# Layer 1 attention: the transposes of the last task's exponentials move ahead of this task's scores in each unit

## The chip, the cores and the metric

The kernel runs on one core of a Trainium2 chip. The metric is the device time of one execution in microseconds (us), measured outside the profiler; the profile is a separate execution of the same program.

## What is computed

A two-layer decoder over x of 64 sequences x 128 positions x 256 features. Layer 0 is a state-space block, a cross attention and a recurrent cell; layer 1 is a self attention, a second cross attention over `ctx_1024`, and a mixture of 8 experts with a shared expert. Only the self attention of layer 1 is touched:

```python
def _L1_attn_ref(x, w_q, w_k, w_v, w_o, g):      # x: the layer-normed input
    x_norm = _rms_norm(x, g)
    q = (x_norm @ w_q)...   # 16 heads of 16
    k = (x_norm @ w_k)...   # 4 key heads, each shared by 4 query heads
    v = (x_norm @ w_v)...
    qkt = einsum('brkqa,bkca->brkqc', q5 * rf, k * rf) / 16
    attn = softmax(qkt, axis=-1)
    s = einsum('brkqc,bkca->brkqa', attn, v)
    o = s @ w_o
    return s + o
```

## The kernel before

The 64 sequences are 16 groups of four. The program runs in four phases, each with its own on-chip buffers: the state-space block; cross attention and recurrence of layer 0; everything of layer 1 up to the routing (the phase of this change, called phase three here); the experts. All data are 32-bit floats.

In phase three, work is written as generators that yield. `run_units` (L62 on) keeps them in a heap ordered by (unit, priority, index). A generator that yields `(n, p)` is resumed n units later with priority p; within a unit the lower number goes first, and with equal numbers the older task. Inside `tc.manual_schedule` the order in which instructions are issued is the order in which each of the four compute engines executes them, so priorities are the instruction order of every engine. There is no other reordering.

One attention task is one sequence (b) and one half of its heads (c = 0 or 1): 8 heads, in two halves i of four heads. A new task begins every unit, so in every unit five tasks are at five different steps. What one unit U issues for attention, in the order before, by priority:

- 0: for a c = 1 task four units old, ScalarE copies `prs` out of PSUM (L324); for the task beginning now with c = 0, GpSimd builds the block-diagonal keys `kbd` (L349).
- 1: the task two units old. TensorE makes the scores `s0` and `s1` (L264), VectorE their row maxima `mx0` and `mx1` (L270), ScalarE the four exponentials of half 0 with their row sums (L282, here "e0").
- 2: for older c = 1 tasks VectorE adds the output to x (L335, odd units) or makes `oT` (L327, even units); then, for the task three units old, TensorE transposes the exponentials of the last unit, `pt0` and `pt1` (L294, 4 transposes each), ScalarE copies `pt0` to `eT0` (L296), VectorE copies `pt1` to `eT1` (L298), and in odd units VectorE takes the reciprocal of the row sums (L301) and ScalarE spreads it as `rd` (L303). This is the block that the change moves.
- 4: ScalarE's four exponentials of half 1 for the task two units old (L282, "e1").
- 5 and 6: the other work of the phase ("fill" below): the norms, projections and transposes of a group's inputs (`self_inputs`), the second cross attention and the routing (`cross_and_route`), and scatters of rows to DRAM (L958).
- 7: in even units TensorE's output projection `pr` (L331), which needs `oT`.
- 8: TensorE's attention-times-values `av` (L312), 16 small matmuls that need `eT0` and `eT1`; in odd units two transposes of `rd` behind it (L319).

The fill repeats every 8 units, one group. Units are named u0 to u7 below, by unit number modulo 8. The PSUM banks that matter, `s0`, `s1`, `pt0`, `pt1` and `av`, have one buffer each: the new `s1` must wait until the e1 of the task before has read it. The score matmuls of the two halves use 64 rows of the TensorE array each, rows 0 to 63 and 64 to 127.

`attention` is also used by the cross attention of layer 0 in phase two, with its own priorities for the fill.

Of the kernel before, what the change touches and what calls it, by code (L numbers as in the profile page):

```python
# [46 lines left out]
def last(ap, n):  # L47

    shape = list(ap.shape)
    return ap.unsqueeze(len(shape)).to_broadcast(shape + [n])  # L50
# [28 lines left out]
def tile_decoder(ctx: ExitStack, tc: tile.TileContext, a: dict, out: bass.AP):  # L79
# [13 lines left out]
    def load_rows(pool, name):  # L93

        return load(pool, name, a[name].rearrange("(c p) m -> p c m", p=P))
# [155 lines left out]
                start=(k == 0), stop=(k == 1),  # L251
            )

    def attention(g, b, c, work, ps, got, q, keys, values, wo):

        kb = keys()
        yield 2, 1
        ss = [ps.tile([P, 4, P], F32, tag=f"s{i}", name=f"s{i}") for i in range(2)]  # L260

        for i in range(2):
            rows = slice(i * 64, i * 64 + 64)
            nc.tensor.matmul(  # L264
                ss[i], lhsT=q()[rows], rhs=kb[rows, :, :], start=True, stop=True
            )

        mx = [work.tile([P, 4], F32, tag=f"mx{i}", name=f"mx{i}", bufs=2) for i in range(2)]
        for i in range(2):
            nc.vector.tensor_reduce(mx[i], ss[i], AX.X, ALU.min)  # L270
        e, eT = (
            [work.tile([P, 4, P], F32, tag=f"{n}{i}", name=f"{n}{i}", bufs=2) for i in range(2)]
            for n in ("e", "eT")
        )
        if c == 0:
            got["den"] = work.tile([P, 16], F32, tag="den", name="den", bufs=4)
        den = got["den"]

        def exponentials(i):
            for h in range(4):  # L280
                at = c * 8 + i * 4 + h
                nc.scalar.activation(  # L282
                    e[i][:, h, :], ss[i][:, h, :], AF.Exp, bias=mx[i][:, h:h + 1], scale=-1.0,
                    accum_out=den[:, at:at + 1],
                )

        exponentials(0)
        yield 0, 4
        exponentials(1)
        yield 1, 2  # L290
        for i in range(2):
            pt = ps.tile([P, 4, P], F32, tag=f"pt{i}", name=f"pt{i}")
            for h in range(4):
                nc.tensor.transpose(pt[:, h, :], e[i][:, h, :], ident)  # L294
            if i == 0:
                nc.scalar.copy(eT[i], pt)  # L296
            else:
                nc.vector.tensor_copy(eT[i], pt)  # L298
        if c == 1:

            nc.vector.reciprocal(den, den)  # L301
            rd = work.tile([P, 16, 16], F32, tag="rd", name="rd", bufs=2)
            nc.scalar.copy(rd, last(den, 16))  # L303
        yield 0, 8

        if c == 0:
            got["av"] = ps.tile([P, 4, P], F32, tag="av", name="av")
        av = got["av"]
        for odd in range(2):
            for j in range(4):  # L310
                h = 2 * j + odd
                nc.tensor.matmul(  # L312
                    av[j * 32:j * 32 + 32, c, :],
                    lhsT=values(h), rhs=eT[h // 4][:, h % 4, :], start=(odd == 0), stop=(odd == 1),
                )
        if c == 1:

            for k in range(2):
                nc.tensor.transpose(  # L319
                    av[:, 2 + k, :], rd[:, 8 * k:8 * k + 8, :].rearrange("p h e -> p (h e)"), ident  # L320
                )
            yield 1, 0
            prs = work.tile([P, 2, P], F32, tag="prs", name="prs", bufs=2)
            nc.scalar.copy(prs, av[:, 2:4, :])  # L324
            yield 0, 2
            oT = work.tile([P, 2, P], F32, tag="oT", name="oT", bufs=2)
            nc.vector.tensor_tensor(oT, av[:, 0:2, :], prs, ALU.mult)  # L327
            yield 0, 7
            pr = ps.tile([P, T], F32, tag="mm", name="pr")
            for k in range(2):  # L330
                nc.tensor.matmul(  # L331
                    pr[:, :D], lhsT=oT[:, k, :], rhs=wo[:, k, :], start=(k == 0), stop=(k == 1)
                )
            yield 1, 2
            nc.vector.tensor_tensor(X[g][:, b, :], pr[:, :D], X[g][:, b, :], ALU.add)  # L335

    def values_of(work, n, i):

        v = work.tile([P, n, 64], F32, tag=f"v{i}", name=f"v{i}")
        nc.gpsimd.memset(v[:, :, 16:48], 0.0)  # L340
        return v
# [5 lines left out]
    def block_diagonal(work, k, mask, bufs):  # L347
        kb = work.tile([P, 4, P], F32, tag="kbd", name="kbd", bufs=bufs)
        nc.gpsimd.tensor_tensor(out=kb, in0=mid(k, 4), in1=last(mask, P), op=ALU.mult)  # L349
        return kb  # L350
# [211 lines left out]
    with phase_pool("work1", "left") as work, phase_pool("ps1", space=PSUM) as psp:  # L562
        ps = PsumPool(psp, {"mm": 8})
        got = {}
# [13 lines left out]
    lwq, lwk, lwv, lwo = (load_rows(w3, n) for n in ("lwq", "lwk", "lwv", "lwo"))  # L578
# [82 lines left out]
    def cross_attention(g, b, c, work, ps, got):  # L661
        tb = slice(b * P, (b + 1) * P)
        v = got["v"][(g * G + b) % 3]
        yield from attention(
            g, b, c, work, ps, got, lambda: got[g, "qT"][c][:, tb],
            lambda: block_diagonal(work, got[g, "kT"][c][:, tb], turned, 3),
            lambda h: v[:, 4 * c + h // 2, h % 2 * 32:h % 2 * 32 + 32], xwo,
        )
# [60 lines left out]
    with phase_pool("work2", "left") as work, phase_pool("ps2", space=PSUM) as psp:  # L729
        ps = PsumPool(psp, {"mm": 3, "s0": 1, "s1": 1, "pt0": 1, "pt1": 1, "av": 1})  # L730
        got = {"c2": c2, "v": [values_of(work, 8, i) for i in range(3)]}
# [72 lines left out]
    def self_attention(g, b, c, work, ps, got):  # L804
        qT, kT, v = got[g]
        tb = slice(b * P, (b + 1) * P)

        def keys():
            if c == 0:
                got["k", b] = block_diagonal(work, kT[:, tb], head, 3)  # L810
            return got["k", b]

        yield from attention(
            g, b, c, work, ps, got, lambda: qT[:, c, tb], keys,
            lambda h: v[:, b * 2 + h % 4 // 2, h % 2 * 32:h % 2 * 32 + 32], lwo,
        )

    def wide_attention(g, work, ps):
# [207 lines left out]
    with phase_pool("work3", "left") as work, phase_pool("ps3", space=PSUM) as psp:  # L1026
        ps = PsumPool(psp, {"mm": 3, "s0": 1, "s1": 1, "pt0": 1, "pt1": 1, "av": 1})
# [31 lines left out]
        for k in range(2):  # L1059
# [5 lines left out]
        got = {"full": base, "v": [values_of(work, G * 2, i) for i in range(2)]}  # L1065
        tasks = [(8 * g, 5, self_inputs(g, work, ps, hc, got)) for g in range(NG)]
        tasks += [(8 * g + ATTEND + 11, 5, cross_and_route(g, work, ps, got)) for g in range(NG)]
        tasks += [
            (8 * g + ATTEND - 2 + 2 * b + c, 0, self_attention(g, b, c, work, ps, got))
            for g in range(NG) for b in range(G) for c in range(2)  # L1070
        ]
# [8 lines left out]
    with phase_pool("work4", "left") as work, phase_pool("ps4", space=PSUM) as psp:  # L1080
        ps = PsumPool(psp, {"mm": 5, "dn": 3})
# [323 lines left out]
```

## Time and profile before

| what | value |
|---|---|
| median of 3 executions | 3118.29 us (3117.29 to 3120.63) |
| the profiled execution, its own time | 3180.57 us |
| its span, first to last instruction | 3178.8 us |
| mean granted TensorE clock in it | 0.968 |
| TensorE busy, whole span | 94% |
| VectorE, ScalarE, GpSimd busy | 60%, 59%, 44% |
| first score matmul of phase three | at 1819.1 us |
| last exponentials of its attention | at 2644.2 us |

The profiled execution is 62 us longer than the median. In the profile each row names an engine (PE is TensorE, PEld its weight loads, DVE is VectorE, ACT is ScalarE, POOL is GpSimd), a source line, the tile written and the tiles read. A wait is written as the idle time of an engine and the instruction whose end released it. A matmul's record lasts until its result is out, which overlaps the next matmul, so distances between starts are used for TensorE and not the durations.

### The profile page before, as it was taken

The page shows a single profiled execution, that of the slowest core. Times are in us where ns is not written, and L with a number is a line of the kernel's source. Part 1 is how long each engine was busy: PE and PEld are TensorE (multiplying, and loading weights), DVE is VectorE, ACT ScalarE, POOL GpSimd, SP SyncE. Part 2 cuts the span into 40 slices and gives each one's busy share as a digit, 9 for nine tenths or more (in the row PEclk, how much of TensorE's full clock was granted, in tenths as well). Part 3 has the DMA queues.
Part 4 walks back from the last instruction along what each step waited for, and adds up shares of the span by engine and source line. Part 5 has one row for each costly group of instructions (what it writes and reads, how often), then busy time and mean ns, then how long its engine had stood idle before and what let it go on. Part 6 is the DMA issues. An engine that isn't in the chain of part 4 may idle for free.

```text
span 3178.8 us, 54631 instructions
## 1 busy us (share of the span) xinstructions
PE 2984.9 (94%) x19022; PEld 2042.6 (64%) x19022; DVE 1892.9 (60%) x4891; ACT 1861.4 (59%) x6757; POOL 1406.1 (44%) x1268
## 2 busy tenths in 40 slices
PE   7999999996999999999999699999999997899884
PEld 3666666653777777777777456666666665688542
DVE  5677777753555555555555367777777774433344
ACT  3655555543677667766776277777777773233100
POOL 2667766674434343334332222434342422333554
PEclk8999999998999999999999799999999998899897
DMA  9990000001111111111110100111111111677443
GB/s 309 343 343 32 1 1 1 1 15 52 35 29 33 39 36 29 33 39 36 31 32 21 43 14 28 59 43 61 41 61 41 54 41 50 227 226 222 125 157 120
DMA packets 192245, 246.60 MB, mean 78 GB/s; under 512 B 24672, under 2 KB 156256, under 8 KB 191968
## 3 DMA queue, kind: packets, MB, share of 16 engines
q1 hardware_dynamic: 174000, 196.92, 19.9%
q0 software_dynamic: 17968, 46.18, 4.7%
q8 instruction: 150, 2.46, 0.3%
q14 instruction: 127, 1.04, 0.1%
HBM read 113.65 MB, written 127.93 MB: 76 GB/s over the span
## 4 chain that ended last, share of the span: by engine, by line
PE 75%; ACT 9%; DVE 6%; POOL 4%; issue 3%; another core or an unknown queue 1%; DMA 1%; SPq 0%; DVEq 0%; ACTq 0%; POOLq 0%
PE proj L241 17%; PE s L264 8%; PE pt L294 6%; PE pu L695 5%; PE pu L691 5%; PE av L312 4%; PE pgu L1198 4%; ACT e L282 4%; PE seg L519 2%; PE po L546 2%; PE pr L331 2%; PE pv L249 2%; PE py L531 2%; PE pd L1207 2%; ACT xn L215 2%
## 5 line engine op out<-in xcount | busy, mean ns | idle before, releaser
L282 ACT ACTIVATE e<-s,mx 128x128 f32<-128x128 f32 x2048 | 738.4, 396 | 382.4 <-DVE mx L270 382.4
L270 DVE TENSOR_REDUCE mx<-s 128x4 f32<-128x512 f32 x512 | 331.4, 684 | 462.7 <-PE s L264 452.4
L282 ACT ACTIVATION_READ_ACCUMULATOR e<-s,mx 128x1 f32 x2048 | 479.5, 234 | 0.0
L189 POOL TENSOR_TENSOR ln_rstd<-ln_ve,neghalf 128x4 f32<-128x4 f32 x80 | 82.0, 1025 | 698.1 <-DVE ln_ve L205 558.2
L264 PE MATMUL s<-kbd,qT 64*128 64x512 f32 x1024 | 333.3, 649 | 18.5 <-POOL qT L631 8.6
L294 PEld LDWEIGHTS pt<-consts,e 128*128 128x128 f32 x2048 | 220.8, 141 | 194.5 <-issue 145.2
L241 PE MATMUL proj<-xnT,win 128*128 128x512 f32 x640 | 303.0, 610 | 0.0
L294 PE MATMUL pt<-consts,e 128*128 128x128 f32 x2048 | 281.5, 281 | 0.0
L423 DVE SCALAR_TENSOR_TENSOR acc<-proj,convw,acc 128x508 f32<-128x508 f32 (+2 forms) x288 | 211.6, 735 | 61.9 <-ACT acc L414 59.5
L691 PE MATMUL pu<-xnTb,fx 128*128 128x128 f32 x1536 | 235.6, 276 | 1.2 <-DVE xnTb L682 1.2
L695 PE MATMUL pu<-c,fu 128*128 128x128 f32 x1536 | 234.5, 275 | 1.8 <-DVE c L726 1.8
L691 PEld LDWEIGHTS pu<-xnTb,fx 128*128 128x128 f32 x1536 | 208.0, 192 | 31.3 <-issue 23.9
L349 POOL TENSOR_TENSOR kbd<-kT,consts 128x512 f32<-128x512 f32 x192 | 202.3, 1064 | 4.7 <-PE s L264 4.1
L695 PEld LDWEIGHTS pu<-c,fu 128*128 128x128 f32 x1536 | 202.4, 192 | 2.4 <-DVE c L726 2.4
L241 PEld LDWEIGHTS proj<-xnT,win 128*128 128x128 f32 x640 | 115.1, 193 | 112.9 <-issue 108.0
L312 PE MATMUL av<-eT,v 128*32 128x128 f32 x4096 | 165.8, 280 | 12.7 <-ACT eT L296 12.5
L298 DVE COPY eT<-pt 128x512 f32<-128x512 f32 x256 | 174.2, 680 | 4.8 <-PE pt L294 4.8
L630 POOL TENSOR_TENSOR other<-other,consts 128x512 f32<-128x512 f32 x64 | 81.4, 1271 | 198.6 <-DMA other<-raw 198.6
L1261 POOL DMA_INDIRECT ys<-ys,t_yrow x128 | 123.6, 966 | 90.8 <-DVE x L1271 40.9
L189 POOL TENSOR_TENSOR rn_rstd<-ln_ve,neghalf 128x1 f32<-128x1 f32 x64 | 37.2, 581 | 278.3 <-ACT prs L324 190.6
L526 POOL TENSOR_TENSOR m<-m,gm 128x1024 f32<-128x1024 f32 x64 | 151.0, 2360 | 15.8 <-ACT m L520 15.8
L312 PEld LDWEIGHTS av<-eT,v 128*32 128x32 f32 x4096 | 96.7, 109 | 95.4 <-issue 33.0
(280 smaller groups left out, 6531.4 us busy)
## 6 DMA issues: line engine op xcount, KB each, us to landing
xs<-zeros SPq DMA_DIRECT2D x64, 1024.0 KB
xs<-xs SPq DMA_DIRECT2D x71, 256.0 KB
ys<-y SPq DMA_DIRECT2D x71, 256.0 KB
ctxT<-in_ctxT_dram SPq DMA_DIRECT2D x32, 512.0 KB
other<-raw SPq DMA_DIRECT2D x256, 64.0 KB
x<-in_x_dram SPq DMA_DIRECT2D x16, 512.0 KB
xo<-xo SPq DMA_DIRECT2D x64, 128.0 KB
xo<-xo SPq DMA_DIRECT2D x16, 512.0 KB
```

The lines of the kernel that those rows point to most:

```text
L241: nc.tensor.matmul(o[:m, :], lhsT=w[:, k, m0:m0 + m], rhs=rhs[k], start=(k == 0), stop=(k == 1))
L264: nc.tensor.matmul(ss[i], lhsT=q()[rows], rhs=kb[rows, :, :], start=True, stop=True)
L270: nc.vector.tensor_reduce(mx[i], ss[i], AX.X, ALU.min)
L282: nc.scalar.activation(e[i][:, h, :], ss[i][:, h, :], AF.Exp, bias=mx[i][:, h:h + 1], scale=-1.0, accum_out=den[:, at:at + 1],)
L294: nc.tensor.transpose(pt[:, h, :], e[i][:, h, :], ident)
L298: nc.vector.tensor_copy(eT[i], pt)
L312: nc.tensor.matmul(av[j * 32:j * 32 + 32, c, :], lhsT=values(h), rhs=eT[h // 4][:, h % 4, :], start=(odd == 0), stop=(odd == 1),)
L349: nc.gpsimd.tensor_tensor(out=kb, in0=mid(k, 4), in1=last(mask, P), op=ALU.mult)
L423: nc.vector.scalar_tensor_tensor(acc[:, :, k:], pv[:, :, :P - k], convw[:, conv, 3 - k:4 - k], acc[:, :, k:], ALU.mult, ALU.add,)
L526: nc.gpsimd.tensor_tensor(out=m, in0=m, in1=mid(gm, 8), op=ALU.mult)
L691: nc.tensor.matmul(pu[:, i, :], lhsT=fx[:, k, m], rhs=xnT[:, k, :], start=(k == 0), stop=False)
L695: nc.tensor.matmul(pu[:, i, :], lhsT=fu[:, k, m], rhs=got["c2"][:, k, :], start=False, stop=(k == 1),)
```

## The change

`attention` gets an argument `turn`, the priority of the block with the transposes. Layer 0 keeps 2. Layer 1 passes 0.5, so in each unit of phase three the block of L294 to L303 is issued after priority 0 and ahead of the scores (1).

```diff
-    def attention(g, b, c, work, ps, got, q, keys, values, wo):
+    def attention(g, b, c, work, ps, got, q, keys, values, wo, turn=2):
...
         exponentials(0)
         yield 0, 4
         exponentials(1)
-        yield 1, 2
+        yield 1, turn
         for i in range(2):
             pt = ps.tile([P, 4, P], F32, tag=f"pt{i}", name=f"pt{i}")
...
         yield from attention(
             g, b, c, work, ps, got, lambda: qT[:, c, tb], keys,
-            lambda h: v[:, b * 2 + h % 4 // 2, h % 2 * 32:h % 2 * 32 + 32], lwo,
+            lambda h: v[:, b * 2 + h % 4 // 2, h % 2 * 32:h % 2 * 32 + 32], lwo, 0.5,
         )
```

The instructions and their number stay the same. By engine, the order at the head of a unit changes like this:

| engine | before | after |
|---|---|---|
| TensorE | s0 s1, pt0 pt1, fill, pr (even), av | pt0 pt1, s0 s1, fill, pr (even), av |
| VectorE | mx0 mx1, x add or oT, eT1, reciprocal (odd), fill | eT1, reciprocal (odd), mx0 mx1, x add or oT, fill |
| ScalarE | prs (even), e0, eT0, rd (odd), e1, fill | prs (even), eT0, rd (odd), e0, e1, fill |
| GpSimd | unchanged | unchanged |

No DMA is moved, and no queue of DMA issues.

## The prediction

> **What bounds the kernel now.** The page's first part says that TensorE is busy nearly throughout, so the question is what little idle time it has in phase three. The busy table by stretches narrows it: at a granted clock of 1.00, TensorE is busy 78.6 of 80 us, ScalarE only 60 to 64.
>
> ```profile
> PE 2984.9 (94%) x19022; PEld 2042.6 (64%) x19022; DVE 1892.9 (60%) x4891; ACT 1861.4 (59%) x6757; POOL 1406.1 (44%) x1268
> ```
> ```profile
> 2220.00:2300.00 80.00, 78.62 (x560) 50.24 (x560) 60.47 (x180) 60.36 (x260) 28.29 (x24) 1.00 0.14 46
> 2300.00:2380.00 80.00, 78.66 (x568) 51.36 (x567) 64.04 (x193) 64.29 (x270) 35.32 (x31) 1.00 0.17 57
> ```
>
> Busy hides stalls inside stretched records, so I then read the waits of the weight loads from 1900 to 2630 us (total, times, longest). `s` waits for the exponentials, which is the bank of s1; `av` waits for eT.
>
> ```profile
> PEld av L312 <- ACT eT L296: 19.9, 30, 1.0
> PEld s L264 <- ACT e L282: 16.0, 30, 0.5
> PEld av L312 <- ACT rd L303: 10.6, 14, 0.8
> ```
>
> The timeline shows how such a wait acts. First TensorE around u6 and u7 (start, length; I use distances between starts):
>
> ```profile
> 2335.93 0.44 PE L319 MATMUL av<-consts,rd 128*128 128x128 f32 x2
> 2336.30 1.13 PE L264 MATMUL s<-kbd,qT 64*128 64x512 f32 x4
> 2337.36 1.09 PE L294 MATMUL pt<-consts,e 128*128 128x128 f32 x8
> 2338.29 1.04 PE L227 MATMUL pt_ln<-consts,xn 128*128 128x128 f32 x8
> 2339.51 1.13 PE L331 MATMUL pr<-lwo,oT 128*128 128x256 f32 x4 [0.18 <-DVE oT L327]
> 2340.93 0.65 PE L312 MATMUL av<-eT,v 128*32 128x128 f32 x16 [0.29 <-ACT eT L296]
> 2341.50 1.96 PE L264 MATMUL s<-kbd,qT 64*128 64x512 f32 x4
> 2343.39 1.09 PE L294 MATMUL pt<-consts,e 128*128 128x128 f32 x8
> ```
> ```profile
> 2342.33 0.29 PEld L264 LDWEIGHTS s<-kbd,qT 64*128 64x128 f32 x2 [0.54 <-ACT e L282]
> ```
>
> In u6 both score halves take 1.06 together, because they run in different rows. In u7 s1 may not start until e1 of the last task is read; s0 runs alone, s1 runs alone behind it, and the pair takes 1.89. pt takes 0.93. From the end of e1's last read (2341.95 + 0.33 = 2342.28, ScalarE's timeline) to the fill at 2344.32 TensorE needs 2.04 us: 0.05 + s1 1.06 + pt 0.93. A period of 8 units is 52.8 us, and it has three stretched pairs: u3 (2315.89, 1.89), u4 (2322.34, 1.45), u7 (2341.50, 1.89). In u1 to u4 and from u5's e0 to u7, ScalarE runs without a gap and TensorE follows it; in between TensorE is the bound.
>
> **What the change does, part by part** (the profiled period from 2303.78 to 2356.59).
>
> 1. The scores no longer meet a bank in use: pt1 comes first and waits for e1, and once it has run both score banks are free, so the pair always takes 1.06. pt1 waits by head: the same kind of transpose, pt_ln, runs three of its four and waits only for the slice still missing:
>
> ```profile
> 2312.32 0.70 PE L227 MATMUL pt_ln<-consts,xn 128*128 128x128 f32 x3
> 2313.18 0.76 PE L227 MATMUL pt_ln<-consts,xn 128*128 128x128 f32 x5 [0.16 <-ACT xn L215]
> ```
>
> So behind e1 there is left: 0.05, one weight load 0.14 (mean of the L294 loads), one transpose 0.12 (0.93 / 8), a switch of 0.10 (point 5), the pair 1.06: 1.47 instead of 2.04, a gain of 0.57. If pt1 had to wait with all four heads, 0.35 of that is lost (0.22 left). It counts at u4 and u7: 2 x 0.57 = 1.14. At u3 I count nothing, because ScalarE goes on with `xnr` to 2318.4, which u3's transposes need anyway.
>
> 2. eT0 (0.47) and rd (0.31) leave the chain between e0 and e1. In u5 they move into idle time, and e0 pays for the later mx:
>
> ```profile
> 2331.70 0.37 ACT L282 ACTIVATE e<-s,mx 128x128 f32<-128x128 f32 x1 [2.59 <-DVE mx L270]
> 2333.09 0.60 ACT L296 COPY eT<-pt 128x512 f32<-128x512 f32 x1
> 2333.55 0.43 ACT L303 COPY rd<-den 128x256 f32<-128x256 f32 x1
> ```
>
> e0 begins 1.94 after the unit (2329.76); with pt ahead it is 1.94 + 0.93 + 0.10 = 2.97. 1.03 later less 0.78 gives e1 0.25 later. This goes through ScalarE's unbroken work in u6 to u7: loss 0.25. In u1, mx is held by VectorE's own fill (e0 at 2306.27): eT1 and the reciprocal, 0.76, now stand before it, and 0.78 leaves ScalarE: nothing. With that cover gone u1 would lose up to 0.76 more.
>
> 3. av no longer waits for eT0 or rd, which are 1 to 2 us earlier. Where it waited (u2, u6) the next unit's e1 wait follows, so nothing is counted; this stall becomes pt1's wait. Bounds: nothing, and 0.3 per period.
>
> 4. VectorE in even units: oT now follows eT1, mx0 and mx1, and `pr`, `av` and the next unit are queued behind oT on TensorE. From scores to the next scores: 1.16 (to mx0) + 1.20 (both mx) + 0.49 (oT to pr) + 0.95 + 0.58 + 0.93 + 0.10 = 5.41. In u6 the scores would start at 2336.75, so this path ends at 2342.16; that of e1 (2342.28 - 0.57 + 0.25, then 0.41 to the scores) at 2342.37. It is hidden by 0.2; without that cover it costs what it exceeds. GpSimd's keys come a unit or more early (2329.83 for 2341.50); it is 30 to 40% busy: nothing.
>
> 5. Order on TensorE itself. The Trainium skill, "TensorEngine Tiling (Array Packing)", Key Properties, speaks against the change: a change of the tiling mode drains the array. av is tiled by columns, the scores by rows, transposes by neither. In odd units the number of changes stays three; in even units av, s, pt, fill becomes av, pt, s, fill: four instead of three. The rows give a price: two transposes ahead of scores take 0.37 (2335.93 to 2336.30), where 8 of them ahead of full matmuls take 0.87 (u3), 0.22 for two: 0.15 for the change. pt behind scores takes 0.93 against 0.87: 0.06. I take 0.10. By the rule alone, all four even units would pay up to 0.15, 0.6 per period; by the rows only the TensorE-bound u0 pays beyond points 1 and 2: 0.10. pt straight ahead of scores appears nowhere in the trace; bounds 0 and 0.4 a unit.
>
> Sum per full period: 1.14 - 0.25 - 0.10 = 0.79 us. Full periods run from 1927.9 to 2560.9: twelve, 9.5 us. The period before them has two stretched pairs: 0.5.
>
> 6. The thin units 17 to 22, early in the phase, have almost no fill and are bound by the loop itself:
>
> ```profile
> 1853.35 1.96 PE L264 MATMUL s<-kbd,qT 64*128 64x512 f32 x4
> 1858.27 1.96 PE L264 MATMUL s<-kbd,qT 64*128 64x512 f32 x4
> 1862.98 1.74 PE L264 MATMUL s<-kbd,qT 64*128 64x512 f32 x4
> ```
>
> They take 4.7 to 4.9 now. After: odd 1.94 + 2.80 (8 exponentials) + 0.41 = 5.15, even 5.41, mean 5.28 against 4.81: 6 x 0.47 = 2.8 us lost. The last ten units, partly thin, have both effects; I count nothing.
>
> Total: 9.5 + 0.5 - 2.8 = 7.2 us against the profiled 3180.57. These stages ran at full clock, so I take the same 7.2 from the median: 3118.3 - 7.2 = 3111.
>
> **The rivals.** About 0.2% (6.2 us) is what a measurement of this kernel can tell from no change.
>
> A, the forecast: 3111, chance 0.5. Its own range: with 0.3 from point 3 and u3's pair counted in part (0.3), 1.4 per period, 14.5 in all: 3104. With u5's loss doubled, 0.54 per period: 3114.
>
> B, no change, 0.28: the stall is only renamed. pt1 waits with all four heads (gain 0.22 twice, less 0.35: 0.09 per period, 1.1) and the thin units take 2.8 back: 3120. For it: the exponentials still gate the same engine. Against: the two rows of pt_ln.
>
> C, slower, 0.22: the drain of transposes straight ahead of row-tiled scores. Place: L294 to L264, every unit. Price: 0.4 instead of 0.10, 0.3 more in the five TensorE-bound units (u4, u5, u7, u0, u1), 1.5 per period; 0.79 - 1.5 = -0.7, times 12 is -8.5, with the thin units (2.8 and 1.8 more for the drain) -13: 3131. It decides from 0.16 us above my 0.10 in each of the five; slower by over 0.2% from about 0.2 above. For it: the skill's rule, and that no row shows this pair. Against: 0.15 in the nearest row.
>
> That the change does nothing is excluded: it reorders three queues that run in order.
>
> **How the numbers follow.** A holds 0.48 faster and 0.02 same, B 0.23 same, 0.03 faster and 0.02 slower, C all slower: faster 0.51, same 0.25, slower 0.24. The range reaches from A's best, 3102 with the last units gaining, to 3127, which cuts C's far half.
>
> **What would show it.** Right: the pair takes 1.06 in every unit; PE's wait on e1 stands at pt with 1.5 from e1's end to the fill in u4 and u7; av's waits for eT and rd are gone; period 52.0; thin units near 5.3. Wrong: s starts over 1.1 after pt (C); pt1's four heads run together behind e1 (B); oT ends last in u6; u1's exponentials start late because eT1 stands ahead of mx.

## The result, and the profile after

The kernel after takes 3124.36 us (median of 20 executions, 3118.23 to 3129.35), the kernel before on the same chip 3119.59 (3117.29 to 3121.57): ratio 1.0016, interval 1.0009 to 1.0022. The forecast was 3111, so the sign is wrong; the time itself lies inside the stated range. The profiled execution of after took 3121.84, its span is 3120.1.

The page's first part and the busy table of the same two stretches as before (us, busy of TensorE, weight loads, VectorE, ScalarE, GpSimd, clock, DMA share, GB/s):

```profile
PE 2954.1 (95%) x19022; PEld 2025.4 (65%) x19022; DVE 1903.0 (61%) x4891; ACT 1872.9 (60%) x6757; POOL 1410.6 (45%) x1268
```
```profile
2220.00:2300.00 80.00, 77.83 (x564) 49.82 (x564) 63.35 (x182) 62.64 (x266) 28.70 (x24) 1.00 0.14 46
2300.00:2380.00 80.00, 77.70 (x569) 50.20 (x568) 65.16 (x193) 64.64 (x270) 35.50 (x31) 1.00 0.18 57
```

TensorE was busy 78.6 of 80 us here and is now busy 77.7 to 77.8, with some more matmuls in each stretch. It stalls less inside its records and more between them. The waits of its weight loads from 1900 to 2630 us say on what:

```profile
PEld pr L331 <- DVE oT L327: 15.3, 16, 2.5
...
PEld pt L294 <- ACT e L282: 8.1, 40, 0.2
...
PEld proj L241 <- DVE x L335: 5.4, 13, 0.7
```

The scores' wait for e1 (16.0 us in 30 waits before) is not in the list any more; the transposes' wait for e1 that takes its place is never longer than 0.2. The lines of av's waits for eT0 (19.9 us) are gone and those for rd (10.6) are down to one of 0.3. Idle time of the weight loader alone does not show that TensorE stood still, but here its matmuls agree: `av` now starts 1.06 after `pr`, where it was 1.42. Two waits for VectorE have grown: new is, in each u3, that of a projection for the x add of L335, and that of `pr` for oT was in the list of before with

```profile
PEld pr L331 <- DVE oT L327: 6.3, 14, 0.9
```

TensorE around u6 and u7, as shown of before:

```profile
2337.08 1.13 PE L264 MATMUL s<-kbd,qT 64*128 64x512 f32 x4
2338.14 1.09 PE L227 MATMUL pt_ln<-consts,xn 128*128 128x128 f32 x8
2339.91 1.13 PE L331 MATMUL pr<-lwo,oT 128*128 128x256 f32 x4 [0.68 <-DVE oT L327]
2340.97 0.65 PE L312 MATMUL av<-eT,v 128*32 128x128 f32 x16
2341.55 1.09 PE L294 MATMUL pt<-consts,e 128*128 128x128 f32 x8
2342.57 1.13 PE L264 MATMUL s<-kbd,qT 64*128 64x512 f32 x4
2343.63 1.12 PE L241 MATMUL proj<-xnT,lwq 128*128 128x512 f32 x2
```

The score pair of u7 takes 1.06 (2342.57 to 2343.63) instead of 1.89. The last read of e1 ends at 2341.86 + 0.33 = 2342.19 (ScalarE's timeline), so from there to the fill it is 1.44 us: 1.47 was predicted, 2.04 it was. A period of eight units takes 52.51 us instead of 52.81. That is a gain of 0.30 where 0.79 was predicted, 3.0 us over the thirteen periods from unit 25 to unit 129 (681.99 to 679.01, units counted from the start of the phase); the ends of the phase lose more than that.

### The profile page after: what moved, and what is told of

It reads as the page before. It is cut to its first block, busy times and chain, and to the rows that moved or that the text cites. A ratio compares the mean times of both kernels' runs of the same rounds, so it can differ in the third digit from the quotient of the medians.

```text
span 3120.1 us, 54702 instructions
## 1 busy us (share of the span) xinstructions
PE 2954.1 (95%) x19022; PEld 2025.4 (65%) x19022; DVE 1903.0 (61%) x4891; ACT 1872.9 (60%) x6757; POOL 1410.6 (45%) x1268
## 3 DMA queue, kind: packets, MB, share of 16 engines
q14 instruction: 127, 1.03, 0.1%
## 4 chain that ended last, share of the span: by engine, by line
PE 82%; DVE 6%; POOL 4%; ACT 4%; issue 3%; DMA 1%; SPq 1%; POOLq 0%; ACTq 0%; DVEq 0%
PE proj L241 17%; PE s L264 9%; PE pt L294 8%; PE pu L695 6%; PE pu L691 6%; PE av L312 4%; PE pgu L1198 4%; PE pr L331 4%; PE pv L249 4%; PE seg L519 2%; PE po L546 2%; PE py L531 2%; PE pd L1207 2%; PE pxo L249 2%; DVE mx L270 2%
## 5 line engine op out<-in xcount | busy, mean ns | idle before, releaser
L282 ACT ACTIVATE e<-s,mx 128x128 f32<-128x128 f32 x2048 | 730.3, 394 | 288.9 <-DVE mx L270 285.4
L264 PE MATMUL s<-kbd,qT 64*128 64x512 f32 x1024 | 297.4, 651 | 15.8 <-POOL qT L631 8.6
L294 PEld LDWEIGHTS pt<-consts,e 128*128 128x128 f32 x2048 | 224.8, 141 | 122.2 <-issue 101.3
L294 PE MATMUL pt<-consts,e 128*128 128x128 f32 x2048 | 285.7, 280 | 2.9 <-ACT e L282 2.3
L296 ACT COPY eT<-pt 128x512 f32<-128x512 f32 x256 | 159.3, 622 | 50.9 <-PE pt L294 50.0
L704 ACT ACTIVATE th<-pu,fb 128x128 f32<-128x128 f32 x384 | 115.4, 379 | 65.8 <-PE pu L695 65.8
```

The lines of the kernel that those rows point to most:

```text
L264: nc.tensor.matmul(ss[i], lhsT=q()[rows], rhs=kb[rows, :, :], start=True, stop=True)
L282: nc.scalar.activation(e[i][:, h, :], ss[i][:, h, :], AF.Exp, bias=mx[i][:, h:h + 1], scale=-1.0, accum_out=den[:, at:at + 1],)
```

## The experiments

Chips differ: the kernel before was measured again beside each batch of runs, and took 3120 us in three of the batches (the result above; runs 1 to 4; runs 13 to 16) and 3172 to 3178 in the other three (runs 5 to 8; 9 to 12; 17 and 18). They are called the 3120 chips and the 3175 chips below. Times are compared as ratios to the kernel before on the same chip, and traces by distances inside phase three. The runs are numbered in the order of their texts here. Two theories stood at the start: the thin units and the last units lose more than the full periods gain (so the old order there brings the gain out), or TensorE pays more for the order itself (so the loss is in the full periods too). A third one came out of run 5.

**The control, and the thin units apart.** First a second profile of the kernel before, then the old order in the first units, then the new order there alone:

```diff
-  ... lwo, 0.5,
+  ... lwo, 2 if g == 0 or (g == 1 and b == 0) else 0.5,     # run 2
+  ... lwo, 0.5 if g == 0 or (g == 1 and b == 0) else 2,     # run 3
```

> The kernel before again, unchanged, for a second profile, because its first profile carries long waits on an unknown queue near the end of phase three (7.1 us) and in the last phase. Theory clock (TensorE loses its full clock in the thin units 17 to 22 of the changed kernel and not before the change): no stretch at half clock between the first scores of phase three plus 25 us and the last scores. Theory switches (only the order on TensorE costs): the same trace. Both: a period of 52.8 us, first scores to unit 25 about 66.7 us.

> The block keeps priority 2 in the thin units (blocks in units 14 to 23) and has 0.5 from unit 24 on. Theory clock: the thin units' loss, larger in unprofiled runs than in the profile, is gone, the full periods' gain of 0.3 each stays: 3116 us, with a scatter as small as that of before (4 us). Theory switches (the loss lies in the full periods of the unprofiled runs, the thin units cost only the 0.8 us of their loop): 3123 to 3124, scatter as after.

> The mirror of it: priority 0.5 in the thin units alone, 2 from unit 24 on. Theory clock: 3125 to 3128 with the wide scatter of after (some 10 us), a stretch at half clock among units 17 to 22 of the profile. Theory switches: 3120 to 3121, scatter of before.

The control, a single execution on a 3120 chip, took 3121.17. Run 2: 3119.46, ratio 0.9996 (0.9989 to 1.0002), period 52.51. Run 3: 3122.78, ratio 1.0007 (0.9999 to 1.0015), period 52.85. From the scores of unit 13, with which the phase's attention begins, to those of unit 25 the control takes 65.65, run 3 67.34: the new order costs this stretch 1.7 us. The thin units are 5.10 long in odd and 5.49 in even units (before: 4.92 and 4.71). The 1.7 leans on the control: the clock is at half when the phase starts, and in unit 14 the control takes 7.06, but the profile of before and seven more of the old order take 8.01 or 8.02, with a mean clock of 0.50 in it instead of 0.58. Against those the loss would be 0.6. The profile of after takes 70.86 over the same stretch. 1.02 of that is only that its scores stand 1.02 later in their unit; 2.3 is one unit, unit 20, of 7.82 us instead of 5.49, and the busy table (columns as above) shows why, for after and for run 3:

```profile
1857.00:1865.00 8.00, 6.27 (x31) 3.13 (x32) 2.79 (x8) 3.95 (x20) 4.13 (x5) 0.57 0.00 0
```
```profile
1857.00:1865.00 8.00, 5.92 (x57) 3.10 (x53) 5.02 (x13) 5.14 (x25) 5.29 (x4) 1.00 0.00 0
```

The granted clock fell to half for 6.8 us, and 31 instead of 57 matmuls were run. This is not peculiar to one execution: the profiles of runs 9, 10 and 13, which have the same order in these units and were taken on chips of both kinds, show the same unit at 7.83 and the same 6.8 us at half clock. In each of the four it comes 30.7 us after the clock had come back to full at the start of the phase. In run 3, with the same order up to unit 23, the clock came back after 13.7 us at half and not after 10.2, and did not fall again. What makes it fall is not shown. The last units are the other half of what the ends cost: from unit 129 to unit 140 the control takes 64.82, run 2 and after 66.72: 1.9 us.

**Odd units only; full periods only.**

```diff
+  ... lwo, 0.5 if c == 1 else 2,                            # run 4
+  ... lwo, 0.5 if (1, 1) <= (g, b) and g < NG - 1 else 2,   # run 5
```

> The block has 0.5 only for tasks with c = 1, so only in odd units; even units keep scores first and so have three changes of tiling on TensorE as before. Theory switches: units u0 and u4 are back at 6.97 and 7.03 plus at most 0.05, the odd ones keep 0.05 more, the stretched pair of u7 is gone and that of u4 stays; period 52.5 to 52.7, thin units shorter than in after; 3117 to 3120. Rival oT path (the even units are held by oT and not by the order): u2 and u6 fall from 5.5 to 5.2 or less between scores and TensorE waits for e1 instead.

> Priority 0.5 only in the full periods (blocks from unit 24 to unit 133), 2 in the thin units at both ends. Theory ends (the full periods gain 0.3 each and the thin units at both ends give it back, at the start partly by a half clock): period 52.5, first scores to last exponentials 3 us shorter than before, 3116 to 3118. Theory full periods (unprofiled runs lose inside the full periods): not faster than before, 3120 to 3124.

Run 4: 3119.88, ratio 0.9999 (0.9990 to 1.0007), with executions from 3112 to 3126; its profile has a period of 52.30: odd units alone gain 0.51 a period, more than all units together, and the time does not show it. Run 5: ratio 1.0017 (1.0009 to 1.0026), where the thin units keep the old order and nothing should lose. Its period is 53.12 instead of 52.51, and all of the difference is in u3, which takes 7.18 instead of 6.57. So the same code has two lengths of u3. That was not in any of my theories; it is clearest in a second profile of the kernel after itself (below, run 9).

**u3, u4 and u7 apart.**

```diff
+  ... lwo, 0.5 if c == 1 and b in (0, 2) and 0 < g < NG - 1 else 2,                      # run 6
+  ... lwo, 0.5 if (b, c) in ((0, 1), (2, 1), (3, 0)) and 0 < g < NG - 1 else 2,          # run 7
```

> Priority 0.5 only in u3 and u7 of the full groups, where the score pair was stretched to 1.89 us; all other units keep the order of before. Theory switches (each extra change of tiling on TensorE costs 0.1 to 0.2 us in a unit where TensorE is the bound, and moving the block pays only where e1 is waited for): u1 and u5 are back at 6.54 as seen from fill to fill, period 51.8 to 51.9, 12 us faster than before, 3108 to 3110. Rival oT path (the gain comes from the block being early everywhere, because eT and av are early): period no shorter than with all odd units, 52.2, 3113 or more.

> As the one before, and u4 too, whose pair took 1.45 us. Theory switches: 0.39 of stretch against 0.2 of an extra change: period 51.6 to 51.8, 3106 to 3109. If u4 is not held by e1 any more once u3 has moved: 0.2 longer per period than without u4.

Ratios 0.9992 (0.9981 to 1.0003) and 0.9994 (0.9983 to 1.0005), periods 52.78 and 52.87, where 51.6 to 51.9 was expected. In run 6, from fill to fill, the steps of u6 and u7 together gain 0.54, those of u2 and u3 together lose 0.51: u7 gains and u3 loses as much. But this loss is the second length of u3 again. In the second and third full period, where VectorE's copy in u3 is on time, u2 and u3 take what they take in before (12.29 and 12.27 in the third); from the fourth on the copy is 0.9 late and they take 12.77 to 12.95 for 12.26 to 12.42. So by these two periods u3's block, moved together with u7's alone, costs nothing by itself.

**Dummy transposes against the half clock** (run 8). After, with ten transposes of the identity behind the scores of the first and last units, whose results nothing reads.

```diff
+        if warm:
+            pw = ps.tile([P, 4, P], F32, tag="mm", name="pwarm")
+            for j in range(warm):
+                nc.tensor.transpose(pw[:, j % 4, :], ident, ident)
```

> The changed kernel with ten extra transposes of the identity behind the scores in the thin units (tasks of group 0 from its third sequence, the first sequence of group 1, and group 15); their result is read by nobody. Theory clock: no stretch at half clock between units 17 and 23 nor among the last attention units, 2 to 3 us faster than the changed kernel without them (3121 to 3122), scatter halved. Theory loop only (the thin units lose by their chain and not by the clock): 3124 to 3125 with the scatter of after.

Ratio 1.0032 (1.0023 to 1.0042). The half clock did not appear in the thin units: from unit 13 to unit 25 it is 69.47 us in this profile, 70.83 in that of after on another of the 3175 chips (run 9). The kernel after was not measured on this chip, so what the dummies are worth in the time stays open.

**Who holds VectorE's copy in u3.** After again (run 9), and (runs 10 to 12) the scatters of a group's last three sequences one unit later, in the new order, in the old order and in that of run 6:

```diff
-                yield 1, 6
+                yield (2 if b == 0 else 1), 6
```

> The changed kernel again, beside the next three. Theory port (in u3 the copy eT1 on VectorE, now at the head of the unit, races with the second scatter of the unit before on GpSimd; where the scatter starts first, eT1 waits about 1 us until it ends): the period is either 52.5 us (eT1 of u3 starts at once) or 53.1 us (it starts 0.9 to 1.0 us late), and the time is 4 or 10 us above before accordingly. Theory clock and switches alone: always 52.5.

> The changed kernel with the second to fourth pair of row scatters of a group issued one unit later, so that no scatter stands at the head of u3 on GpSimd. Theory port: eT1 of u3 starts at once and the period is 52.5 or less on any chip; against the changed kernel without the shift 0 us where that already had 52.5, 7 us less where it had 53.1 (twelve periods of 0.6). Theory without port: no difference to the changed kernel.

> The control: the order of before with the same shift of the scatters. Theory port: eT1 of u3 does not wait in before (it comes behind both mx), so the shift gives nothing: within 2 us of before, period 52.8. If the shift is worth something by itself: faster than before by more than 3 us.

> Priority 0.5 only in u3 and u7 of the full groups, with the shift of the scatters. Theory switches and port: period 51.9 to 52.2, no loss in the thin units, 7 to 11 us faster than before. If the gain of u3 and u7 needs the other units too: period 52.5 or more, 3 us at most.

Ratios: after 1.0029 (1.0015 to 1.0044), shifted after 1.0078 (1.0061 to 1.0096), shifted before 1.0059 (1.0045 to 1.0073), shifted run 6 1.0049 (1.0036 to 1.0062). On this chip after lost more than in the result above, and its period was 53.06. Compare one u3 in the two profiles of the same kernel, VectorE first, of the profile that goes with the result:

```profile
2369.32 0.69 DVE L298 COPY eT<-pt 128x512 f32<-128x512 f32 x1 [0.80 <-PE pt L294]
...
2370.37 1.29 DVE L270 TENSOR_REDUCE mx<-s 128x4 f32<-128x512 f32 x2 [0.20 <-PE s L264]
2371.58 0.41 DVE L335 TENSOR_TENSOR x<-pr,x 128x256 f32<-128x256 f32 x1
```

and of the second profile, whose scores of this unit start at 2374.35 (those above at 2369.21):

```profile
2375.38 0.69 DVE L298 COPY eT<-pt 128x512 f32<-128x512 f32 x1 [1.71 <-PE pt L294]
...
2376.14 1.22 DVE L270 TENSOR_REDUCE mx<-s 128x4 f32<-128x512 f32 x2
2377.28 0.41 DVE L335 TENSOR_TENSOR x<-pr,x 128x256 f32<-128x256 f32 x1
```

The copy eT1 starts 0.11 after the scores in the first and 1.03 after them in the second, and maxima, x add and projection come late with it. "PE pt" is named as the releaser, but the transposes were as early as in the first. GpSimd in the two profiles:

```profile
2369.35 0.96 POOL L958 DMA_INDIRECT xs<-xnr,r_rows  x1 [0.30 <-issue]
```
```profile
2374.49 0.96 POOL L958 DMA_INDIRECT xs<-xnr,r_rows  x1 [0.30 <-issue]
```

Both scatters start 0.14 after the scores. In the first profile the copy was 0.03 us ahead and ran beside the scatter; in the second it starts when the scatter is over (2374.49 + 0.96 = 2375.45, within 0.07). It looks like a race for the first start, but the other periods speak against that. In the first profile again, another u3, where the scatter is 0.11 ahead of the copy:

```profile
2054.27 0.69 DVE L298 COPY eT<-pt 128x512 f32<-128x512 f32 x1 [0.94 <-PE pt L294]
```
```profile
2054.16 0.96 POOL L958 DMA_INDIRECT xs<-xnr,r_rows  x1 [0.30 <-issue]
```

Both run at their usual length. In the first full period with scatters of the second profile, the scatter starts 0.21 after the scores, 0.10 after the moment at which the copy starts elsewhere, and the copy is held all the same, to 1.05. What does divide the profiles is the chip: in those of after and run 2, on 3120 chips, the copy is on time in all eleven u3 with a scatter beside them; in those of runs 5, 8 and 9, on 3175 chips, it is late in all eleven. What differs between these chips is not shown. The weight load of the projection in the second profile waits 0.92 us for the x add, 0.35 in the first:

```profile
2377.74 0.30 PEld L241 LDWEIGHTS proj<-xnT,ym 128*128 128x128 f32 x2 [0.92 <-DVE x L335]
```

The Trainium skill, "SBUF — State Buffer", section "SBUF: two separate sides", has a rule that comes to mind: VectorE and GpSimd share a pair of ports by an exclusive lock, and whichever starts first keeps it for its whole instruction. The page names the VectorE instructions that take it: those in a mode that uses two ports, or with two inputs in SBUF against a GpSimd instruction that reads SBUF. The copy has one input, in PSUM, so by the page alone it is not expected to be held; and the order of starting does not decide here. So what holds it is not shown to be this lock.

The shift did take the scatter out of u3: shifted after has u3 at 6.56 again, on the same chip where unshifted after has 7.12. This pair of runs shows that the scatter holds the copy. But it pushed GpSimd's unbroken chain further into u5 and u6, with an instruction of VectorE on the other side of it (VectorE, then GpSimd, shifted after):

```profile
2402.27 3.90 DVE L212 SCALAR_TENSOR_TENSOR ln_off<-ln_mv,ln_inv 128x4 f32<-128x4 f32 x1
```
```profile
2403.78 2.36 POOL L766 TENSOR_TENSOR xo<-xo,hc 128x1024 f32<-128x1024 f32 x1
```

The tiny L212, 0.16 us in most units of the trace of after, lasts 3.90 and ends with GpSimd's addition (2406.17 and 2406.14); it has two inputs in SBUF and the addition reads SBUF, which is a pair that the page's rule names. If it is that lock, GpSimd kept it over three instructions in a row, since the record of L212 begins inside a scatter (2401.80 to 2402.77). eT1 and oT of u6 come 1.7 us later for it, and u6 takes 7.60 instead of 5.49; the old order with the shift has the same (6.94 instead of 5.20). So the shift moved one collision and made a larger one, in every order, and the times of these runs do not tell what u3 is worth.

**Without scatters, u7 alone, and all but u3.** All on one 3120 chip. Runs 13 and 14 leave the scatters out, in the new and the old order, so that no routed row is written and the experts see none.

```diff
-                nc.gpsimd.indirect_dma_start(out=XV..., in_=xn[:, b, :], in_offset=None)   # runs 13, 14
+  ... lwo, 0.5 if c == 1 and b == 0 and 0 < g < NG - 1 else 2,                            # run 15
+  ... lwo, 2 if (b, c) == (2, 1) else 0.5,                                                # run 16
```

> The kernel after with the row scatters of the routing (L958) left out: the routed rows are not written, so the experts compute on rows without tokens. Race theory (eT1 at the head of u3 waits for a scatter that GpSimd started just before): without scatters eT1 in u3 starts 0.04 us after pt1 in every period, u3 takes 6.57 us, a period 52.5, and the ratio to the same kernel in the old order (the run without scatters of the kernel before) is 0.999 to 1.001. Order theory (the loss comes from the order of TensorE and the thin units alone): period 53.1 as in the last profiles of the kernel after, ratio to the old order without scatters 1.003.

> The control: the kernel before with the same scatters left out (the routed rows are not written). Both theories: period 52.8, as with them, since in the old order no copy waits for a scatter; GpSimd's time falls by 128 instructions of about 1 us, and the time falls by at most a few us at the end of the phase.

> Only the block of u7 (c = 1, b = 0) of the full periods goes ahead of the scores. Race theory: u7 is free of scatters and has the larger part of the gain; the pair of u7 goes from 1.9 to 1.06, the period from 52.8 to 52.3 (0.53 from fill to fill), twelve or thirteen times: -6 us, ratio 0.998. Rival (a stall removed in u7 is only moved to the next u1 or u3): period 52.7 to 52.8, ratio 0.9995 to 1.0005.

> The kernel after with the block of u3 alone (b = 2, c = 1) back in its old place. Race theory: no copy stands ahead in the unit that has the scatter in front, so the period is 52.4 to 52.7 in every profile instead of 53.1 where the race is lost, and the time is about 6 us under that of the kernel after on a chip where it loses, ratio 1.000 to 1.001. Order theory: u3 was one of the units that gained, so the period is 53.1 or more and the ratio 1.003 or more.

| run | median us | ratio to before (interval) | period |
|---|---|---|---|
| 13, after without scatters | 3123.00 | 1.0009 (1.0001 to 1.0018) | 52.50 |
| 14, before without scatters | 3122.88 | 1.0010 (1.0003 to 1.0017) | 52.71 |
| 15, u7 alone | 3113.22 | 0.9981 (0.9972 to 0.9989) | 52.25 |
| 16, all but u3 | 3115.49 | 0.9982 (0.9976 to 0.9989) | 52.05 |

Without scatters eT1 starts 0.04 us after its transposes in every u3, u3 takes 6.56, and the two orders differ by 0.1 us, each to about 0.08%. For the scatter this is no further evidence, since in the profiles of the moved u3 on 3120 chips (after, run 2) u3 takes 6.56 with scatters too. That the old order did not get faster without the scatters, but 0.1% slower, was not expected and stays unexplained.

Run 16 is the one that surprised: its period is 0.46 shorter than that of after *with no collision in either trace*. So moving u3's block cost time from the start, and the scatter only adds to it. TensorE's weight loads in u3, of after:

```profile
2370.27 0.31 PEld L227 LDWEIGHTS pt_ln<-consts,xnr 128*128 128x128 f32 x3 [0.76 <-ACT xnr L215]
2370.80 0.14 PEld L227 LDWEIGHTS pt_ln<-consts,xnr 128*128 128x128 f32 x1 [0.22 <-ACT xnr L215]
2371.28 0.42 PEld L227 LDWEIGHTS pt_ln<-consts,xnr 128*128 128x128 f32 x4 [0.34 <-ACT xnT L229]
2372.05 0.30 PEld L241 LDWEIGHTS proj<-xnT,ym 128*128 128x128 f32 x2 [0.35 <-DVE x L335]
```

and of run 16:

```profile
2365.51 0.90 PEld L227 LDWEIGHTS pt_ln<-consts,xnr 128*128 128x128 f32 x8
2366.38 0.30 PEld L241 LDWEIGHTS proj<-xnT,ym 128*128 128x128 f32 x2
```

In the old order the transposes `pt` stand between the scores and this fill, just while ScalarE makes `xnr` and VectorE the maxima and the x add; when the fill comes, everything is ready and nothing waits. In the new order `pt` is done ahead, and the fill, straight behind the scores, waits twice for ScalarE (0.22 and 0.34) and then for the x add. (The 0.76 of the first line is no wait of TensorE's: the loader is idle that long while a pair of scores runs, in u3 of before too.) From the first of these transposes to the projection it is 1.77 us in after and 0.87 in run 16. The x add ends 1.16 + 1.21 + 0.41 = 2.78 us after the scores (to the maxima, the two maxima, the add), and the projection starts at 2.84. VectorE's copy is not in the way there: in the lines of u3 above it is over at 2370.01, and the maxima wait for the scores until 2370.37. From the end of e1 of u2 (where `xnr` begins) to the projection it is 3.45 in after and 3.12 in run 16 and before.

**TensorE's transposes alone, and the version the findings point to.** Run 17 moves only the transposes and leaves eT0, eT1, the reciprocal and rd in their old places; run 18 moves all but u3, in the full periods.

```diff
+        pt = [ps.tile([P, 4, P], F32, tag=f"pt{i}", name=f"pt{i}") for i in range(2)]     # run 17
+        for i in range(2):
+            for h in range(4):
+                nc.tensor.transpose(pt[i][:, h, :], e[i][:, h, :], ident)
+        if turn < 1:
+            yield 0, 2
+        nc.scalar.copy(eT[0], pt[0])
+        nc.vector.tensor_copy(eT[1], pt[1])
...
+  ... lwo, 0.5 if 0 < g < NG - 1 else 2,                                                  # run 17
+  ... lwo, 0.5 if 0 < g < NG - 1 and (b, c) != (2, 1) else 2,                             # run 18
```

> In the full periods only, TensorE's transposes alone go ahead of the scores; the copies eT0 and eT1, the reciprocal and rd stay where they were, behind the maxima and e0. VectorE theory (the gain of the score pairs is given back where eT1 and the reciprocal stand ahead of work that TensorE waits for: the x add in u3, oT in u2 and u6, and a scatter that blocks eT1): u3 starts its projection without a wait for the x add, no copy meets a scatter, u6 is under 5.4 us, and the period is 52.2 or less. Rival (what costs is that TensorE's scores come 1 us later, so that maxima and exponentials come later, whatever VectorE does): eT0 and rd now stand between e0 and e1 again, 0.78 us more in odd units, and the period is 52.8 or more.

> Every block of the full periods but that of u3 goes ahead of the scores; the first and last group and u3 keep the old order. By the trace of the kernel with only u3 put back the period is 52.05, so over twelve periods 0.75 x 12 = 9 us less than before, less some 0.5 us at the ends: ratio 0.9970 to 0.9976. Rival (what the thin units lost was in part lost by the full units around them): ratio 0.998, as with u7 alone.

Run 17: ratio 1.0061 (1.0047 to 1.0075), period 54.24. The theory that VectorE's copy ahead of the maxima is what costs foresaw 52.2 or less and fell; its rival, 52.8 or more, held. With no copy ahead the projection of u3 waits for the x add all the same. This u3 is not a clean case, since on this 3175 chip the maxima behind a scatter are late too, 1.61 after the scores (at 2379.73) instead of 1.16:

```profile
2381.34 1.29 DVE L270 TENSOR_REDUCE mx<-s 128x4 f32<-128x512 f32 x2 [2.34 <-PE pt_ln L227]
```

Most of the loss is elsewhere. With the copies behind, oT and eT0 are later still (TensorE in u6 of run 17, scores at 2346.31):

```profile
2349.48 1.13 PE L331 MATMUL pr<-lwo,oT 128*128 128x256 f32 x4 [1.01 <-DVE oT L327]
2350.90 0.65 PE L312 MATMUL av<-eT,v 128*32 128x128 f32 x16 [0.29 <-ACT eT L297]
```

`pr` starts 3.17 after the scores instead of 2.83, av another 1.42 later instead of 1.06, and u6 takes 6.25. So the copies early are a help that the new order needs. That what costs in it is the shorter stretch of work between the scores and whatever waits for their maxima rests on the lines of u3 above; no run adds other work there to test it.

Run 18: 3163.16 against 3171.93, ratio 0.9973 (0.9962 to 0.9983), period 52.06. It has the lowest ratio of all, some 8.5 us under the kernel before, though its interval overlaps those of runs 15 and 16; its period is that of run 16, which ran on a 3120 chip.

## Why the prediction was wrong, point by point

Steps from one unit's fill to the next one's, in us (TensorE's starts, medians of the profiles; after without a collision):

| | u0 | u1 | u2 | u3 | u4 | u5 | u6 | u7 | period |
|---|---|---|---|---|---|---|---|---|---|
| before (run 1) | 6.97 | 6.54 | 6.40 | 6.02 | 7.03 | 6.54 | 6.03 | 7.29 | 52.8 |
| all but u3 (run 18) | 7.17 | 6.58 | 6.12 | 5.56 | 7.23 | 6.58 | 5.50 | 7.34 | 52.1 |
| after | 7.16 | 6.59 | 5.56 | 6.56 | 7.23 | 6.59 | 5.50 | 7.35 | 52.5 |

The step that failed is point 1's entry for u3: "At u3 I count nothing", beside a full 0.57 for u4. With u3's block moved, u4's gain does not come (from e1's end to its fill 2.04 us before, 2.01 after, 1.47 predicted); with u3's block left, it mostly does (1.58), and the period falls by 0.75 instead of 0.30. These 0.45 a period are 5.9 of the 10 us between the forecast and the sum worked out below.

- **Point 1, the pairs: right in mechanism, wrong at u3.** u7 gained what was foreseen (6.03 to 5.50, and 1.44 for 1.47). "At u3 I count nothing, because ScalarE goes on with `xnr` [...], which u3's transposes need anyway": the row was read rightly, but the conclusion was too kind. `pt` in its old place was the work that covered that wait. Taken away, u3's fill waits and comes late: 52.06 becomes 52.51, 0.45 a period, over half of the 0.79. That is how u4's gain is undone: TensorE itself arrives late there (`pt` at 2374.81, e1's end at 2374.83). The 0.45 holds with the other blocks moved. In run 6, where u4's is not and has no gain to lose, u3's block costs nothing, as was counted.
- **Point 2, e0 and e1.** The 0.25 that u5 was to lose hardly shows: the steps of u6 and u7 together gain 0.49 where all blocks are moved and 0.54 to 0.56 where u5's is not (runs 6 and 15), and u5's own step costs 0.05.
- **Point 3, av.** Its waits are gone. The gains in run 18 (u2, u3 and u6 in the table) are 0.28 + 0.46 + 0.53 = 1.27, where points 1 and 2 left 0.89; the bound of 0.3 given here would explain some of that, but no run separates it.
- **Point 4, VectorE and GpSimd.** The oT path was worked out as 5.41 for an even unit and called hidden by 0.2; u2 and u6 take 5.5 and wait for oT. It did become the bound there, by less than 0.1. The like path in u3, by the x add, was not worked out. "GpSimd [...] is 30 to 40% busy: nothing" failed outright: it asked whether GpSimd is late, not whether one of its instructions lies where VectorE's copy is moved to. Where the copy is held, u3 takes 7.1 instead of 6.57, 0.55 a period, 5.9 us from unit 25 to 129 (679.01 against 684.88 in the second profile). In the profile that goes with the result it is not held, so this is no part of the sum for it.
- **Point 5, tiling changes: mis-sized, if they are what these steps pay for.** 0.10 was priced and counted once, in u0. The steps that only pay are u0 +0.20, u4 +0.20, u1, u5 and u7 +0.04 to 0.05 each: 0.53 a period. One such price is seen directly: `pt` takes 1.02 ahead of scores, 0.93 ahead of fill. The projection in u3 takes 1.91 behind a fill that follows scores, 1.81 where `pt` lies between; so it seems to fall due behind the scores as well, and in u4 too. But in run 4, where only the odd units are moved, u0, u1, u4 and u5 each pay 0.09 to 0.10, where a count of changes had at most 0.05; and no run isolates the tiling from the rest of the order. At most, rival C's cost is there at about a third of the 1.5 a period that C put on it. In run 18 this error and the one under point 3 cancel, and that 0.75 comes out where 0.79 was predicted is luck.
- **Point 6, the ends.** Thin units: 5.10 and 5.49 for 5.15 and 5.41; units 17 to 22 lose 2.2 (run 3: 31.8, control: 29.6) where 2.8 was predicted, and the whole stretch to unit 25 loses 1.7. "The last ten units [...] I count nothing": they lose 1.9. The half clock in the profile of after, 2.3, was not foreseen.

The sum for the profile of after: -3.0 (full periods) + 1.7 + 2.3 (start) + 1.9 (end) = +2.9, measured +4.8 (2.8 to 6.9) on that chip; the rest is open. With u3's copy held, 5.9 more, it would be +8.8; on the 3175 chip of run 9, 0.0029 x 3174 = +9.2 was measured (4.8 to 14.0). That agreement is weak, since the ends are taken from 3120 chips: from unit 129 to unit 140 run 9 takes 77.18 and not 66.72, most of it in the last unit, which takes 12 to 15.5 us on the 3175 chips in every order and 5.7 to 7.2 on the others. The executions of after spread over 11 us and those of before over 4; those of run 16, where u3's copy is not moved, spread over 10, so the copy in u3 need not be what spreads them.

## What to carry to other kernels

An instruction in front of a wait may be the cover of the next wait: before moving it away, write down what TensorE meets next in each unit and when that is ready, also in the units where no gain is expected. When an engine's work is moved in time, lay the other engines' instructions of that moment beside it, whatever their busy share. A gain and a loss in neighbouring units are not to be added one by one: u3's block cost nothing where u4 had no gain to lose. And a reorder that gains in one unit of a period need not be applied to all: with u3 and the thin ends left alone, the same edit gains 0.27%.

## What the runs showed of the hardware

- A scatter issued by GpSimd (0.96 us) can hold a VectorE copy from PSUM for 0.92 us. It did so in all eleven u3 with scatters in each of three profiles on 3175 chips and in none of eleven in each of two on 3120 chips, whichever of the two started first, so that one kernel had periods of 52.51 and 53.06.
- A VectorE instruction of 0.16 us lasted 3.90 us until a GpSimd addition was over; that wait stands in the record's length and not as idle time.
- The granted clock fell to half for 6.8 us in the same short unit in all four profiles of this order (after, runs 9, 10 and 13) and not in that of run 3, whose units there are the same; it cost 2.3 us.
